# A two-layer graph kernel: when row tiles of the last product are finished, and its last transposes in two halves

## The chip, the cores and the metric

The kernel runs on one core of a Trainium2 chip. The metric is device microseconds of one execution; the median of five runs is compared. All data are float32.

## The reference

Two layers over 3327 nodes with 512 features, and one dense matrix `adj` (3327 x 3327):

```python
# layer 0
h = relu(layernorm(x))
q, k, v = h @ Wq.T + bq, h @ Wk.T + bk, h @ Wv.T + bv
x = x + softmax(q @ k.T / sqrt(512) + adj + adj) @ v
# layer 1
h = relu(layernorm(x))
A2 = adj + eye
d = diagonal(A2) ** -0.5
temp = A2 @ h @ W.T
x = x + relu((d[:, None] * A2 * d[None, :]) @ temp)
```

The kernel works out its three large products, (softmax weights) @ h, A2 @ h and A2 @ temp, each as a product of a (3328 x 3328) matrix and a (3328 x 512) one.

## The kernel before, in words

**Tiles.** Rows are padded to 26 tiles of 128. The rows of a result are held in two *strips*: strip 0 has row tiles 0 to 13, strip 1 has 14 to 25; half of a strip (7 or 6 tiles) is `y` = 0 or 1. The 512 feature columns are two halves `z` of 256.

**A product** (three of them, `g` = 0, 1, 2; the change is in the last) is done in two nested levels of a seven-product scheme in the manner of Strassen. The outer level has the seven products of `ORDER = ("p5", "p1", "p6", "p7", "p2", "p3", "p4")`. Each outer product goes over strip 0, then strip 1, and each strip over seven *steps*: `t` = 0 to 5, two tiles of the contraction at once, then `t` = `None`, the odd thirteenth. In the code, `number_of(g, n, s, t)` is the number of a step, with `n` the place in `ORDER`: `n` = 4 is outer p2, 5 is outer p3, 6 is outer p4. A number `t` of 6 is the `None` step, and 7 runs on into the next strip's first step.

Inside a step, `Step.multiply` (L770) issues seven inner products, also called p1 to p7, each into a PSUM bank of its own (`ROLE` has the bank numbers), in the order p6, p7, p5, p2, p3, p4, p1 for `t` = 0 and p1 first otherwise; two matmul records each in the profile, so 14 a step (L782). The `None` step issues p2, p3, p4 and p8 (8 records, L774), and p8 uses p1's bank. `four_sums` (L173 to L175, VectorE) makes the sums of the left operand two steps ahead; `make` (L748, L180 to L183) makes those of the right operand three steps ahead.

**Gathers.** At the end of a strip, VectorE takes the banks' content out: `first` (L810 to L814) after `t` = 5, `rest` (L827 to L830, or L824 for the very last one) at the `None` step, and `settle` (L838 to L843) adds the result to the buffers `ct` of the regions that it belongs to. The next strip's first step needs those banks again.

**Finishing a row tile.** `finish` (L919) transposes the tile's blocks of `ct` on TensorE (L927, four for 512 columns, two for 256) into bank 3, applies the relu with the row's scale on ScalarE (L929), adds the residual `xr` on VectorE (L930) and stores the tile from GpSimd's queue (L92). `finish_load` (L907, L910) fetches `xr`, on ScalarE's DMA queue, one step ahead. `xr` and the output tile come from rings of four buffers. When a tile can be finished follows from the scheme: the second halves (`z` = 1) of tiles 20 to 25 are complete after outer p7, tiles 0 to 6 after outer p3's strip 0, 14 to 19 after its strip 1, 7 to 13 after outer p4's strip 0, and the first halves of 20 to 25 only after the last step of all.

**What sets the order.** The order is written out by hand: `between[k]` holds what is emitted after step `k`, `within[k]` what is emitted after the fourth of its seven products. `in_order` keeps VectorE, TensorE, GpSimd, ScalarE and SyncE each to the order of emission, DMA issues included. `run` (L1012) emits, for one step: the loads of the step three ahead; the products, with `within` in their middle; at a `None` step `rest`; the sums for two steps ahead; after `t` = 5 `first`; after `None` `settle`; then `between`. In the last full step of all, `first` is emitted in the middle, ahead of `within`.

Of the kernel before, what the change touches and what calls it, by code (L numbers as in the profile page):

```python
# [15 lines left out]
P = 128  # L16
# [31 lines left out]
def graph_layers_kernel(  # L48
# [28 lines left out]
    nc = tc.nc  # L77
    N = out.shape[0]
    NP, D = x.shape
    DC = D // P  # L80
# [9 lines left out]
    def store(dst, src, n, queue=nc.gpsimd):  # L90
        for a, z in pieces(n):
            queue.dma_start(dst[a:z], src[a:z])  # L92
# [16 lines left out]
    def bank(k, name):  # L109
        return banks.tile([P, BW], F32, name=name, tag=f"bank{k}")  # L110
# [11 lines left out]
    @contextmanager  # L122
    def in_order(*engines):

        traced = nc.cur_bb.bb.instructions
        before = traced[-1]
        yield
        begin = next(k for k in reversed(range(len(traced))) if traced[k] is before) + 1
        last = {}
        for ins in traced[begin:]:  # L130
            if ins.engine in engines:
                if ins.engine in last:
                    tc.add_manual_dep(ins, last[ins.engine].name,
                                      mybir.DependencyInfo(mybir.DependencyClass.NoSync, mybir.DependencyReason.DATA),
                                      reason="in_order")
                last[ins.engine] = ins
# [5 lines left out]
    ident = const.tile([P, P], F32, name="ident")  # L142
# [88 lines left out]
    class Chain:  # L231
# [32 lines left out]
        @staticmethod  # L264
        def finish():
            if Chain.before:
                Chain.before()
            Chain.before = None
# [34 lines left out]
    ps = [bank(k, "mm") for k in range(DC)]  # L303
# [4 lines left out]
    for r in range(DC):  # L308
        for z in range(2):
            turned = -scale if r < 2 and z == 0 else scale  # L310
# [241 lines left out]
    with in_order(*(e.engine for e in (nc.vector, nc.tensor, nc.gpsimd, nc.sync))):  # L552
# [9 lines left out]
        k = len(steps)  # L562
# [16 lines left out]
    ROLE = {"p1": 0, "p6": 2, "p7": 4, "p5": 6, "p2": 7, "p3": 1, "p4": 5, "p8": 3}  # L579

    def seven():
        return {r: bank(ROLE[r], r) for r in ("p6", "p7", "p5", "p2", "p3", "p4", "p1")}
# [82 lines left out]
    cts = {}  # L665

    def set_up():

        free = [view(k, j)[:, 2 * m : 2 * m + 2] for k, j in ((2, 2), (3, 0), (3, 1), (3, 2)) for m in range(2)]
        free = [f.rearrange("p a w -> p (a w)") for f in free] + [mid(k, [P, H[0]], f"ct{k}") for k in range(10)]  # L670
        for s in range(2):
            cts[s] = [[free.pop()[:, : H[s]] for d in range(DC)] for y in range(2)]
        cts["to"] = [free.pop() for k in range(2)]
# [33 lines left out]
    class Right:  # L707
# [9 lines left out]
        def rows(self, dst, h, z):  # L717

            for k, i in enumerate(self.its):
                src = rowd[self.g][ROW[h * HALF + i]]  # L720
                nc.sync.dma_start(dst[:, k], src if z is None else src[:, z * E : (z + 1) * E])
# [31 lines left out]
    class Step:  # L753
# [8 lines left out]
        def sums(self):  # L762
            for a, d in self.diagonals:
                nc.vector.tensor_add(a, a, d)
            if self.t is None:
                return
            self.o = o_ring3()[:, :, : Q[self.s]]
            four_sums(self.o, self.a.rearrange("p k y w -> p (k y) w"))
# [16 lines left out]
    flags = []  # L785

    class Gather:
# [28 lines left out]
                for o, c, op in zip(self.parts(self.regions[2]), (c11, c12, c21, c22), (ALU.add, ALU.subtract, ALU.add, ALU.add)):  # L816
                    nc.vector.tensor_tensor(o, o, c, op=op)

        def rest(self, ps):
            p = {k: ps[k][:, : self.width] for k in ("p2", "p3", "p4", "p8")}  # L820
            if self.last:
                flags.append(nc.values_load(bad, min_val=0, max_val=1))
                for o, k in zip(self.parts(self.regions[2]), p):
                    nc.vector.tensor_add(o, o, p[k])  # L824
                return
            c11, c12, c21, c22 = self.parts(self.to)
            nc.vector.tensor_add(c11, c11, p["p2"])  # L827
            nc.vector.tensor_sub(c12, p["p3"], c12)
            nc.vector.tensor_add(c21, c21, p["p4"])
            nc.vector.tensor_add(c22, c22, p["p8"])  # L830
# [14 lines left out]
    def where(i):  # L845

        s = int(i >= STRIPS[1])
        return (s, *divmod(i - STRIPS[s], HT[s]))
# [63 lines left out]
    def last_load(i):  # L912

        xr = xr_last([P, 2, E], "xr")
        for k in range(2):
            xrs[i + k] = xr[:, k]
            nc.scalar.dma_start(xr[:, k], x1d[i + k][:, 0:E])

    def finish(i, z=(0, 1), spot=None, queue=nc.gpsimd):  # L919

        s, y, k = where(i)
        n = min(P, N - i * P)
        c0, c1 = z[0] * E, (z[-1] + 1) * E
        xr = xrs[i]
        pt = bank(ROLE["p8"] if spot is None else spot, "pt")
        for d in range(c0 // P, c1 // P):
            nc.tensor.transpose(pt[:, d * P : (d + 1) * P], cts[s][y][d][:, k * P : (k + 1) * P], ident)  # L927
        o = (out_ring if spot is None else out_last)([P, D], "r")
        nc.scalar.activation(o[:, c0:c1], pt[:, c0:c1], AF.Relu, scale=sd[:, i : i + 1])  # L929
        nc.vector.tensor_add(o[:, c0:c1], o[:, c0:c1], xr[:, c0:c1])  # L930
        store(out[i * P : i * P + n, c0:c1], o[:n, c0:c1], n, queue)
# [7 lines left out]
    def number_of(g, r, s, t):  # L939
        return ((g * len(ORDER) + r) * 2 + s) * len(every) + t  # L940

    def at(k, what, *args):
        between.setdefault(k, []).append((what, args))

    early = []
    for g in range(3):
        for n, r in enumerate(ORDER):
            for t, e in enumerate(every):
                k = number_of(g, n, 0, t)
# [9 lines left out]
    for n, job in enumerate(jobs):  # L959
        k = k0 + n * (k1 - k0) // len(jobs)  # L960
# [3 lines left out]
    def rows(g, k, i, *z):  # L964

        if g == 0:
            at(k - 2, attend_load, i)
            at(k, attend, i)
            at(k + 1, attended, i)
        elif g == 1:  # L970
            at(k, temp, i)
        else:
            at(k - 1, finish_load, i, *z)
            at(k, finish, i, *z)
# [3 lines left out]
    for g in range(2):  # L978
        k = number_of(g, 5, 1, 2)
# [4 lines left out]
            k += 1  # L984
    within = {}
    for (n, s, t), its in {
# [3 lines left out]
    }.items():  # L990
        for i, when in zip(its, (between, within)):
            if i is not None:
                k = number_of(2, n, s, t)
                at(k - 1, finish_load, i)
                when.setdefault(k, []).append((finish, (i,)))
    for t, i in enumerate(range(20, NT)):
        rows(2, number_of(2, 4, 0, t), i, (1,))
    for n, i in enumerate(range(20, NT, 2)):
        at(number_of(2, 6, 1, 2) + n, last_load, i)
    for k, what in ((1, totals), (2, prepare), (6, prepared), (8, judge), (9, judged)):  # L1000
# [9 lines left out]
    banks_of, gathers = {}, {}  # L1010

    def run(k):  # L1012
        step = steps[k]
        if k + 3 < len(steps):
            steps[k + 3].load()
        if step.t == 0:
            banks_of.update(seven())
        if not cts:
            set_up()
        if step.t is None:  # L1020
            banks_of["p8"] = bank(ROLE["p1"], "p8")
        t, sums = step.t, steps[k + 2].sums if k + 2 < len(steps) else tuple
        if t == PAIRS - 1:
            gathers[step.r, step.s] = Gather(step.r, step.s, k == len(steps) - 2)
        gatherer = gathers.get((step.r, step.s))
        for j, _ in enumerate(step.multiply(banks_of)):
            if j == 3 and t == PAIRS - 1 and gatherer.last:
                gatherer.first(banks_of)
            for what, args in within.get(k, ()) if j == 3 else ():
                what(*args)  # L1030
        if t is None:
            gatherer.rest(banks_of)
        sums()
        if t == PAIRS - 1 and not gatherer.last:
            gatherer.first(banks_of)
        if t is None:
            gatherer.settle()
        for what, args in between.get(k, ()):
            what(*args)

    with in_order(*(e.engine for e in (nc.vector, nc.tensor, nc.gpsimd, nc.scalar, nc.sync))):
        for k in range(len(steps)):
            run(k)
        for n, i in enumerate(range(20, NT)):
            finish(i, (0,), (0, 2, 4, 6, 7, 1)[n], (nc.gpsimd, nc.sync)[n % 2])
    return flags[0]

@with_exitstack
# [373 lines left out]
```

## Time and profile before

| | us |
|---|---|
| median of 5 runs | 2212.73 (2212.05 to 2215.41) |
| the profiled execution | 2213.48 |
| its span in the profile | 2211.6 |
| outer p2, p3 and p4 of the last product | from about 1985 to 2195 |
| last matmul starts; last DMA issue | about 2194.8; 2199.8 |

The profile is of one execution. PE is TensorE's matmuls, PEld its weight loads, DVE is VectorE, ACT ScalarE, POOL GpSimd, SP SyncE; a q behind the name is the engine's queue of DMA issues. A line of the timeline gives start and length in us, engine, source line, operation, output and inputs, shapes, the number of instructions, and in brackets how long the engine had been idle and what ended that. A line of the table by stretches gives for one stretch of time the busy time of PE, PEld, DVE, ACT and POOL, then TensorE's granted clock (1.00 is full), the busy share of the DMA engines and the GB/s that they moved.

### The profile page before, as it was taken

What the parts mean: (1) busy time and instruction counts of PE and PEld (TensorE: products, weight loads), DVE (VectorE), ACT (ScalarE), POOL (GpSimd) and SP (SyncE); (2) the same over time, 40 slices, a digit from 0 to 9 for tenths busy, and PEclk for the clock granted to TensorE, in tenths of its full rate; (3) what the DMA queues carried; (4) which work ended last, traced back from release to release, by engine and by line L of the source; (5) the groups of instructions that cost most, each with busy time, mean ns of one, the idle gap of its engine ahead of it and who ended that gap; (6) DMA issues with size and microseconds to landing.
All of it is one profiled execution on the core that took longest, in us unless ns stands there. A gap on an engine that the chain in (4) does not pass through costs nothing.

```text
span 2211.6 us, 20973 instructions
## 1 busy us (share of the span) xinstructions
PE 2176.7 (98%) x6268; PEld 1167.8 (53%) x6268; DVE 1627.7 (74%) x3103; ACT 231.0 (10%) x335; POOL 357.4 (16%) x551
## 2 busy tenths in 40 slices
PE   9999999999999999999999999999999999999997
PEld 6555555455555555555454555555545555555554
DVE  6369888888877788877777778886645358777776
ACT  5311121112110000000011000000000000000011
POOL 5233333333321000001222100000000000000001
PEclk9999999999999999999999999999999999999999
DMA  7568888888969898888787899876645458765685
GB/s 288 186 218 300 291 299 285 303 282 312 344 212 321 307 373 298 280 291 314 253 307 266 305 350 353 282 272 201 215 140 188 130 187 302 241 201 182 209 300 170
DMA packets 246682, 583.68 MB, mean 264 GB/s; under 512 B 34768, under 2 KB 106270, under 8 KB 246558
## 3 DMA queue, kind: packets, MB, share of 16 engines
q1 hardware_dynamic: 192270, 399.28, 54.5%
q0 software_dynamic: 44928, 167.49, 19.9%
q10 hardware_dynamic: 9360, 15.47, 2.1%
q8 instruction: 52, 0.85, 0.2%
q14 instruction: 72, 0.59, 0.1%
HBM read 414.28 MB, written 167.85 MB: 263 GB/s over the span
## 4 chain that ended last, share of the span: by engine, by line
PE 88%; DVE 5%; DMA 3%; issue 3%; POOL 1%; SPq 0%; ACT 0%; ACTq 0%; POOLq 0%; DVEq 0%
PE p L782 52%; PE Y L454 13%; PE p L874 7%; PE Z L454 6%; PE p L774 5%; PE X L454 3%; PE Y L347 1%; DVE part L173 1%; DMA b<-row 1%; DMA xt<-in_x_dram 0%; DMA g<-in_adjT_dram 0%; DVE part L174 0%; PE pt L927 0%; DMA p<-g 0%; PE Z L347 0%
## 5 line engine op out<-in xcount | busy, mean ns | idle before, releaser
L782 PE MATMUL p<-part,b 128*128 128x448 f32 (+1 forms) x3528 | 1253.7, 513 | 6.4 <-DVE part L174 4.9
L782 PEld LDWEIGHTS p<-part,b 128*128 128x128 f32 x3528 | 668.4, 190 | 571.0 <-issue 308.3
L173 DVE TENSOR_TENSOR part<-part 128x896 f32<-128x896 f32 (+1 forms) x252 | 257.0, 1020 | 94.9 <-PE p L782 43.9
L454 PE MATMUL Y<-qt,hp 128*128 128x448 f32 (+1 forms) x832 | 309.9, 515 | 4.3 <-DVE g L458 3.3
L454 PEld LDWEIGHTS Y<-qt,hp 128*128 128x128 f32 x832 | 158.4, 191 | 139.7 <-issue 73.5
L454 PE MATMUL Z<-qt,hp 128*128 128x384 f32 (+1 forms) x416 | 162.5, 513 | 0.0
L175 DVE TENSOR_TENSOR part<-part,part 128x448 f32<-128x448 f32 (+1 forms) x219 | 129.5, 591 | 16.9 <-DVE part L174 0.9
L174 DVE TENSOR_TENSOR part<-part,part 128x448 f32<-128x448 f32 (+1 forms) x219 | 129.5, 591 | 7.4
L774 PE MATMUL p<-part,b 128*128 128x448 f32 (+1 forms) x336 | 124.2, 513 | 0.0
L874 PE MATMUL p<-w,ct 128*128 128x512 f32 x272 | 123.5, 593 | 0.5 <-DVE part L886 0.5
L454 PEld LDWEIGHTS Z<-qt,hp 128*128 128x128 f32 x416 | 78.8, 190 | 67.4 <-issue 37.2
L458 DVE SCALAR_TENSOR_TENSOR g<-g,Y 128x384 f32<-128x384 f32 (+1 forms) x156 | 91.3, 586 | 29.1 <-PE Y L454 27.8
L868 POOL DMA_DIRECT2D sum<-job x52 | 28.4, 547 | 501.1 <-DVE job L865 283.5
L811 DVE TENSOR_TENSOR part<-p,part 128x384 f32<-128x384 f32 (+1 forms) x33 | 19.3, 586 | 108.0 <-PE p L782 107.4
L774 PEld LDWEIGHTS p<-part,b 128*128 128x128 f32 x336 | 63.6, 190 | 53.8 <-issue 32.4
L810 ACT COPY part<-p 128x384 f32<-128x384 f32 (+1 forms) x33 | 16.6, 503 | 684.3 <-PE p L782 683.5
L874 PEld LDWEIGHTS p<-w,ct 128*128 128x128 f32 x272 | 51.5, 190 | 59.7 <-issue 51.9
L454 PE MATMUL X<-qt,hp 128*128 128x384 f32 (+1 forms) x208 | 81.1, 512 | 0.0
L461 ACT ACTIVATE g<-g 128x768 f32<-128x768 f32 (+1 forms) x48 | 43.0, 896 | 355.1 <-DVE g L458 297.8
L446 POOL DMA_DIRECT2D sum<-o x52 | 36.9, 709 | 222.8 <-DVE o L440 154.1
L874 PE MATMUL p<-w,part 128*128 128x512 f32 x144 | 65.7, 592 | 0.0
L92 POOL DMA_DIRECT2D out_dram<-r x30 | 16.2, 542 | 304.0 <-DVE r L930 268.9
(165 smaller groups left out, 1878.7 us busy)
## 6 DMA issues: line engine op xcount, KB each, us to landing
part<-sum SPq DMA_DIRECT2D x104, 448.0 KB, 5.0
part<-p SPq DMA_DIRECT2D x91, 448.0 KB, 6.3
part<-sum SPq DMA_DIRECT2D x104, 384.0 KB, 3.4
part<-p SPq DMA_DIRECT2D x91, 384.0 KB, 4.3
part<-in_adjT_dram SPq DMA_DIRECT2D x78, 448.0 KB, 4.9
b<-row SPq DMA_DIRECT2D x234, 128.0 KB, 4.9
part<-in_adjT_dram SPq DMA_DIRECT2D x78, 384.0 KB, 3.7
g<-in_adjT_dram SPq DMA_DIRECT2D x52, 448.0 KB, 4.6
```

Source lines behind the costliest of these rows:

```text
L173: nc.vector.tensor_add(o[:, 0:2], g[:, 0:4:3], g[:, 1:2].to_broadcast([P, 2, g.shape[-1]]))
L174: nc.vector.tensor_add(o[:, 2], o[:, 1], g[:, 0])
L175: nc.vector.tensor_add(o[:, 3], o[:, 2], g[:, 2])
L347: nc.tensor.matmul(ps[:, :w], M[B[name]][:, c, o * P : (o + 1) * P], hp[k][:, A[name], c], start=start and c == 0, stop=c == 1, skip_group ...
L446: nc.gpsimd.dma_start(self.to(sumd)[:, 0:2], self.o)
L454: nc.tensor.matmul(ps[:, :wd], h_of(self.t, name, k), qt[B[name]][:, k], start=start and k == 0, stop=k == 1, skip_group_check=True)
L458: nc.vector.scalar_tensor_tensor(a[n], a[n], 2.0, ps[:, :wd], op0=ALU.mult, op1=ALU.add if sign > 0 else ALU.subtract)
L461: nc.scalar.activation(g[1], g[1], AF.Exp, **({"bias": pad} if self.t == HALF - 1 else {}))
L774: yield nc.tensor.matmul(ps[("p2", "p3", "p4", "p8")[k]][:, :w], b[:, z], a[:, 0, y], start=k == 3, stop=True)
L782: yield nc.tensor.matmul(ps[r][:, :w], b[:, i], m, start=self.t == 0, stop=self.t == PAIRS - 1 and r in ("p1", "p5", "p6", "p7"))
L868: nc.gpsimd.dma_start(sumd[self.s][self.j][:, 2 + self.k], self.a)
L874: nc.tensor.matmul(ps, cts[s][y][d][:, k * P : (k + 1) * P], w[d], start=d == 0, stop=d == DC - 1)
```

## The change

Three edits, all in the last product.

1. The second halves of row tiles 20 to 25 are finished two steps later: at outer p2's strip 0 after steps 2 to 5 and the `None` step, and after the first step of strip 1.
2. The other tiles are finished at other steps. Row tiles by step, with the one after the bar `within` the step and the others after it:

| outer product, strip | before | after |
|---|---|---|
| p3, strip 1 | t2: 0, t3: 1, t4: 2, t5: 3 | t1: 0, t2: 1, t3: 2, t4: 3 \| 4, t5: 5 \| 6 |
| p4, strip 0 | t0: 4, t1: 5, t2: 6 \| 17, t3: 14 \| 18, t4: 15 \| 19, t5: 16 | t1: 14, t2: 15 \| 16, t3: 17 \| 18, t4: 19 |
| p4, strip 1 | t2: 7 \| 8, t3: 9 \| 10, t4: 11 \| 12, t5: \| 13 | t1: \| 7, t2: 8 \| 9, t3: 10 \| 11, t4: 12 \| 13 |

3. The transposes of the last six first halves are taken out of `finish`. `rest` can now do a part of its additions: p2 and p3 first, then the transposes of tiles 20 to 22 (the 384 columns that those two additions complete), then p4 and p8, then the transposes of tiles 23 to 25. The banks that they go to are in the order in which the gather lets go of them: p6, p7, p5, p2, p3, p1, where before it was p1's bank first.

```diff
-        def rest(self, ps):
+        def rest(self, ps, names=("p2", "p3", "p4", "p8")):
             p = {k: ps[k][:, : self.width] for k in ("p2", "p3", "p4", "p8")}
             if self.last:
-                flags.append(nc.values_load(bad, min_val=0, max_val=1))
                 for o, k in zip(self.parts(self.regions[2]), p):
-                    nc.vector.tensor_add(o, o, p[k])
+                    if k in names:
+                        nc.vector.tensor_add(o, o, p[k])
                 return
...
+    def turned(i, z, spot):
+        s, y, k = where(i)
+        pt = bank(spot, "pt")
+        for d in range(z[0] * DC // 2, (z[-1] + 1) * DC // 2):
+            nc.tensor.transpose(pt[:, d * P : (d + 1) * P], cts[s][y][d][:, k * P : (k + 1) * P], ident)
+        return pt
+
+    turned_last = {}
+
+    def turn_last(i):
+        turned_last[i] = turned(i, (0,), LAST[i - 20])
+
+    LAST = tuple(ROLE[p] for p in ("p6", "p7", "p5", "p2", "p3", "p1"))
...
-        pt = bank(ROLE["p8"] if spot is None else spot, "pt")
-        for d in range(c0 // P, c1 // P):
-            nc.tensor.transpose(pt[:, d * P : (d + 1) * P], cts[s][y][d][:, k * P : (k + 1) * P], ident)
+        pt = turned(i, z, ROLE["p8"]) if spot is None else turned_last[i]
...
-        (5, 1, 2): (0,), (5, 1, 3): (1,), (5, 1, 4): (2,), (5, 1, 5): (3,),
-        (6, 0, 0): (4,), (6, 0, 1): (5,), (6, 0, 2): (6, 17), (6, 0, 3): (14, 18), (6, 0, 4): (15, 19), (6, 0, 5): (16,),
-        (6, 1, 2): (7, 8), (6, 1, 3): (9, 10), (6, 1, 4): (11, 12), (6, 1, 5): (None, 13),
+        (5, 1, 1): (0,), (5, 1, 2): (1,), (5, 1, 3): (2,), (5, 1, 4): (3, 4), (5, 1, 5): (5, 6),
+        (6, 0, 1): (14,), (6, 0, 2): (15, 16), (6, 0, 3): (17, 18), (6, 0, 4): (19,),
+        (6, 1, 1): (None, 7), (6, 1, 2): (8, 9), (6, 1, 3): (10, 11), (6, 1, 4): (12, 13),
     }.items():
...
     for t, i in enumerate(range(20, NT)):
-        rows(2, number_of(2, 4, 0, t), i, (1,))
+        rows(2, number_of(2, 4, 0, t + 2), i, (1,))
...
-        if t is None:
+        if t is None and gatherer.last:
+
+            flags.append(nc.values_load(bad, min_val=0, max_val=1))
+            for n, names in enumerate((("p2", "p3"), ("p4", "p8"))):
+                gatherer.rest(banks_of, names)
+                for i in range(20 + 3 * n, 23 + 3 * n):
+                    turn_last(i)
+        elif t is None:
             gatherer.rest(banks_of)
...
         for n, i in enumerate(range(20, NT)):
-            finish(i, (0,), (0, 2, 4, 6, 7, 1)[n], (nc.gpsimd, nc.sync)[n % 2])
+            finish(i, (0,), LAST[n], (nc.gpsimd, nc.sync)[n % 2])
```

The change adds no operation and takes none away: as many matmuls, transposes, additions, loads and stores are issued as before.

More of the change, by code (lines that the diff above doesn't have):

```diff
@@ L917, in last_load @@
             nc.scalar.dma_start(xr[:, k], x1d[i + k][:, 0:E])
+    def turned(i, z, spot):
[8 more added lines that the diff above has]
+    LAST = tuple(ROLE[p] for p in ("p6", "p7", "p5", "p2", "p3", "p1"))
     def finish(i, z=(0, 1), spot=None, queue=nc.gpsimd):
-        s, y, k = where(i)
         n = min(P, N - i * P)
```

## The prediction

> **What bounds the kernel now.** I read the page first: TensorE is busy all but everywhere, so only what removes or adds a TensorE wait, or shortens the tail behind its last matmul, can move the time.
> ```profile
> PE 2176.7 (98%) x6268; PEld 1167.8 (53%) x6268; DVE 1627.7 (74%) x3103; ACT 231.0 (10%) x335; POOL 357.4 (16%) x551
> ```
> Second, the waits of TensorE (us in total, times, longest), of which these three touch the steps that the change edits:
> ```profile
> PE pt L927 <- DVE part L840: 3.1, 2, 2.5
> PE p L782 <- DVE part L827: 1.5, 2, 1.3
> ...
> PE pt L927 <- DVE part L824: 1.1, 1, 1.1
> ```
> Here the transposes of row tile 20 wait for `settle` (L840), matmuls wait for a bank that `rest` has yet to read (L827), and the last transposes wait for the last additions (L824). I call them A, B and C. From 2130 to 2195 us TensorE waits for nothing.
>
> Third, the timeline of TensorE around A (start, length, then idle before in brackets):
> ```profile
> 1985.46 5.42 PE L782 MATMUL p<-part,b 128*128 128x448 f32 x14
> 1991.45 0.33 PE L927 MATMUL pt<-ident,part 128*128 128x128 f32 x1 [0.56 <-DVE part L840]
> 1994.30 0.47 PE L927 MATMUL pt<-ident,part 128*128 128x128 f32 x1 [2.52 <-DVE part L840]
> 1994.57 6.82 PE L782 MATMUL p<-part,b 128*128 128x448 f32 x14
> 2001.23 0.38 PE L927 MATMUL pt<-ident,part 128*128 128x128 f32 x2
> ```
> The 14 matmuls behind the wait take 6.82 us, the 14 before it 5.42. The table by stretches says why (TensorE's clock stands third from the right, at half):
> ```profile
> 1994.00:1997.40 3.40, 3.10 (x5) 1.62 (x6) 3.29 (x8) 0.47 (x1) 0.00 (x0) 0.50 0.42 142
> ```
> Fourth, VectorE and TensorE around B:
> ```profile
> 2117.18 0.69 DVE L930 TENSOR_TENSOR r<-r,xr 128x512 f32<-128x512 f32 x1 [3.53 <-DMA xr<-x1d]
> ...
> 2120.78 0.55 DVE L811 TENSOR_TENSOR part<-p,part 128x384 f32<-128x384 f32 x1
> ...
> 2124.61 0.68 DVE L930 TENSOR_TENSOR r<-r,xr 128x512 f32<-128x512 f32 x1
> 2125.22 0.55 DVE L827 TENSOR_TENSOR part<-part,p 128x384 f32<-128x384 f32 x1
> ```
> ```profile
> 2122.06 2.42 PE L782 MATMUL p<-part,b 128*128 128x448 f32 x6
> 2125.82 1.40 PE L782 MATMUL p<-part,b 128*128 128x448 f32 x3 [1.34 <-DVE part L827]
> ```
> VectorE stood 3.53 us in front of row 2's addition (L930), because `xr` had not landed, and everything queued behind it came late. The landing times of that load, issued by ScalarE's queue, between 2104 and 2121 us:
> ```profile
> DMA to landing us min/median/max: 6.1/6.2/7.2
> ```
> Fifth, the tail:
> ```profile
> 2194.25 1.94 DVE L824 TENSOR_TENSOR part<-part,p 128x384 f32<-128x384 f32 x4
> ```
> ```profile
> 2196.25 1.53 PE L927 MATMUL pt<-ident,part 128*128 128x128 f32 x12 [1.14 <-DVE part L824]
> ```
>
> **A: rows 20 to 25, second half, two steps later.** Undisturbed, these transposes follow each other at 5.48 us (2001.23, 2006.71). Row 20's were due 5.48 - 0.22 us after the step's start at 1985.46, at 1990.7; the next came at 2001.23. That is 10.5 us for a step of 5.48: 5.0 lost, of which 3.1 is idle, 1.5 the halved clock, the rest the stretched transposes. Two steps later `settle` (done at 1994.25) is long past. What is late next: the product p6 of the step after the next needs L174 of its own sums; that ended at 1996.83 and would be wanted at 1996.75, so 0.1 is given back. The six additions, stores and loads move along (0.42 us of VectorE each); in the steps they move to VectorE idled 1.7 to 5.1 us, and the two that cross into the next strip fall ahead of sums that had 2 us to spare. **A: -4.9.**
>
> A rule of the Trainium skill bears on this: "TensorE: Matmul & The Clock Gate", Part 1, puts the fall to half clock behind an idle window of about 3.4 us, and its oscillation section asks for no idle gap above that. This trace is stricter. Elsewhere one gap of 2.91 us was enough:
> ```profile
> 585.00:588.00 3.00, 0.16 (x1) 0.00 (x0) 1.01 (x2) 0.00 (x0) 0.00 (x0) 0.94 0.75 253
> 588.00:591.00 3.00, 2.94 (x5) 1.71 (x6) 2.83 (x6) 1.09 (x2) 1.27 (x2) 0.50 1.05 347
> ```
> By the rule the idle part alone would come back (A = -3.3); by the row 4.9 does. The row decides. But the page also calls the window free-running, so other executions may lose the clock or not: -3.3 and -4.9 are A's ends.
>
> **C: the tail.** Three edits. Row 13 no longer finishes inside the last full step, so its addition (0.6 us, at 2193.65, right ahead of L824) is gone from VectorE there. The additions p2 and p3 now free the first six transposes, which start behind the last matmul (about 2195.0) and not at 2196.25; p4 and p8 end 0.1 to 0.2 us after those six, and ScalarE, which takes 0.36 us a row (2.30 for six), hides that. The other order of banks makes no bank late: those of p6, p7 and p5 are read before `rest` begins. Whatever follows (relus, additions, stores, their landing) only moves forward. Less than nothing is excluded by order, more than 1.3 by TensorE's last matmul. **C: -1.3.** The verdict's load is ahead of the additions in both, at no cost.
>
> **B: rows 0 to 19.** The transposes' sum is the same (0.44 us a row), only their places move. Seven rows, not four, now finish in p3's second strip. I lay TensorE out from its start at 2090.63, with 4.52 us a step (14 records of 0.323): row 0 at 2099.7, row 1 at 2104.6, row 2 at 2109.6; step 4 starts at 2110.0, with row 4 in its middle at 2112.6 and row 3 at 2115.0; step 5 starts at 2115.4, with row 6 at 2118.0 and row 5 at 2120.4; the last step starts at 2120.8; p4's first step at 2123.4, and its product p2 at 2125.65.
>
> The loads: rows 3 and 4 are issued behind row 2's relu (a load follows its transposes by 0.69: 2104.18, 2104.87), at 2110.3 and 2110.7, rows 5 and 6 at 2115.65 and 2116.1. Row 4's and row 6's additions stand *ahead* of their step's sums on VectorE and are ready for relu after less than 4 us, but their loads need more: with 6.2 us row 4 goes at 2116.9, and behind it `make` (1.65) and row 3 (0.6); row 6 then goes at X = 2122.3.
>
> What is queued behind row 6: sums, `first`, `make`, row 5, `rest`. The trace of before has that very sequence: from L930 at 2117.18 to the end of L811 4.15 us, to the end of L827 8.6. Waiting for it is TensorE: bank p6 is free at X + 4.15, bank p2 at X + 8.6.
> - Floor: X = 2119.3, the end of row 6's relu. p6 waits 0.05, p2 2.2: 2.3, against 1.34 today: +0.95.
> - Ceiling: landing in 7.2 us, the worst shown. X = 2123.3; p6 waits 4.05, p2 2.1: 6.2, and with a halved clock (1.5, as in A) 7.7: +6.3.
> - Taken: X = 2121.7. The DMA engines are full here (345 GB/s from 2104 to 2124), which speaks for 6.2; but SyncE's queue holds a `rows` load that waits for VectorE's `make` (L735), so a late VectorE also thins the loads around row 6, and a pair of row loads landed in 5.3 and 5.8 at 2135. 5.6 lies between. p6 waits 2.45, p2 2.15: 4.6. **B: +3.3.** Gaps of 2.45 and 2.15 are shorter than those that halved the clock; I count none.
>
> Behind that, TensorE and VectorE are late together. In p4's first strip the first step has no row now and the second has one for two; I find L174 0.1 us ahead of its matmul in the third step (0.6 today), so no further wait. The loads that SyncE has behind L735 come some 5 us later and had 10 to spare. p4's second strip has VectorE to spare and loads landing in 3.0: nothing.
>
> **Sum.** -4.9 - 1.3 + 3.3 = -2.9. The profiled execution took 2213.48 (span 2211.6), the median is 2212.73; taken from the median, **2209.8 us**.
>
> **The rivals.**
> 1. *Loads land early* (5 us or less; VectorE catches up between rows 4 and 6): B falls to +1 to +2.3, the sum to -5.2 to -3.9: 2207.5 to 2208.8. For it: rows 0 to 2 are out of the way one step sooner. Against: no load in this stretch landed under 6.1. Chance 0.3.
> 2. *The slower side: the addends of rows 4 and 6 hold VectorE.* Two pairs add 512 KB to full engines, at 392 GB/s (2116 to 2120) 1.3 us: landing 8.5, X = 2124.6, waits 7.5, halved clock 1.5: B = +7.7, the sum +1.5: 2214.2. It decides from a landing of about 7.0 us with the clock lost (8.5 without). For it: the 3.53 above is this wait, now twice. To pass 0.2% it would need over 11 us. Chance 0.15.
> 3. *The split doesn't bite*: if p4's addition waits for the first six transposes, which read the same buffers, the second six start 1.0 us later, of which ScalarE's pace hides 0.2: C = -0.5, total 2210.6. Against: in this trace loads go into one half of a buffer while the other is in use. Chance 0.1.
> The likeliest has the remaining 0.45.
>
> About 0.2% (4.4 us) is what a measurement of this kernel can tell from no change. Faster by more asks for a time under 2208.3: rival 1 and an edge of the likeliest, 0.33. Slower by more: the far end of rival 2, 0.08. Within: 0.59. The range, 2206.8 to 2214.0, reaches from rival 1 with a landing at the floor to nearly rival 2, and takes in A's two ends.
>
> **What would show it.** A: no wait of `pt` for L840 and no clock of 0.50 near 1994. C: the last transposes start within 0.2 us of the last matmul. B: VectorE waiting for `xr` before rows 4 and 6, then TensorE waiting twice (for L811, then L827) at the start of p4; their sum is 4.6. Wrong would be: a wait of under 2 there (B too dear), or one of `pt` elsewhere.

## The result and the profile after

The changed kernel took 2210.06 us in the median of 24 runs (2206.78 to 2214.55), the kernel before 2212.6 in the median of 44 beside them: ratio 0.9989, 95% interval 0.9983 to 0.9994. That is 2.5 us, or 0.1%; the forecast was 2.9. The profiled execution took 2212.58 with a span of 2210.4.

In the changed kernel the transposes stand at L923, the relu of a row tile at L940 and its addition at L941. The waits of TensorE from 1970 us to the end:
```profile
PE p L782 <- DVE part L811: 4.0, 1, 4.0
PE p L782 <- DVE part L827: 0.2, 1, 0.2
PE pt L923 <- ACT r L940: 0.2, 1, 0.2
```
The waits A (L840) and C (L824) are gone. B has changed its name, from L827 to L811, and is three times as long.

**A.** The timeline of TensorE where row 20's transposes used to wait:
```profile
1986.20 16.21 PE L782 MATMUL p<-part,b 128*128 128x448 f32 x42
2002.24 0.38 PE L923 MATMUL pt<-ident,part 128*128 128x128 f32 x2
```
42 matmuls, three steps, in one piece: no idle, no slow stretch.

**B.** VectorE in outer p3's last steps and p4's first:
```profile
2115.72 0.69 DVE L941 TENSOR_TENSOR r<-r,xr 128x512 f32<-128x512 f32 x1 [7.35 <-DMA xr<-x1d]
...
2119.71 0.69 DVE L941 TENSOR_TENSOR r<-r,xr 128x512 f32<-128x512 f32 x1 [1.04 <-DMA xr<-x1d]
...
2123.30 0.55 DVE L811 TENSOR_TENSOR part<-p,part 128x384 f32<-128x384 f32 x1
```
The first line is row 4's addition, which kept VectorE waiting for 7.35 us; the second is row 6's, which cost another 1.04. L811, which frees the first bank, came that much later. The loads of `xr`, issued between 2100 and 2116 us:
```profile
DMA to landing us min/median/max: 4.1/6.3/8.0
```
The 8.0 is row 4's. TensorE then:
```profile
2123.91 4.19 PE L782 MATMUL p<-part,b 128*128 128x448 f32 x6 [4.02 <-DVE part L811]
2128.34 8.54 PE L782 MATMUL p<-part,b 128*128 128x448 f32 x22 [0.24 <-DVE part L827]
```
Six records take 4.19 us where they took 2.42, since the clock is halved behind the wait (third figure from the right):
```profile
2124.60:2128.00 3.40, 3.40 (x5) 1.24 (x4) 3.30 (x9) 0.00 (x0) 0.00 (x0) 0.50 0.60 197
```
**C.** The last additions (VectorE), and the last transposes (TensorE):
```profile
2194.91 2.00 DVE L824 TENSOR_TENSOR part<-part,p 128x384 f32<-128x384 f32 x4
```
```profile
2196.15 1.58 PE L923 MATMUL pt<-ident,part 128*128 128x128 f32 x12
```
The transposes now run beside the additions and follow the last matmul without a wait.

**Where the time went.** The `None` steps (L774) cut the trace into stretches that hold the same work in both kernels. From the starts of their matmuls in the timeline, in us:

| kernel | outer p2: 1982.88 to 2053.47 before | p3 strip 1 and p4 strip 0: 2087.62 to 2159.18 before | last `None` step to the end: from 2192.36 before |
|---|---|---|---|
| before | 70.59 | 71.56 | 19.2 |
| changed | 65.83 | 76.80 | 16.8 |
| changed, again | 65.83 | 76.67 | 16.6 |
| A alone | 65.84 | 70.13 | 18.6 |
| split alone | 70.81 | 71.17 | 19.3 |
| table alone | 70.79 | 76.64 | 19.3 |
| A and split, old table | 65.83 | 71.59 | 19.4 |
| loads earlier | 65.82 | 74.25 | 16.9 |
| four rows | 65.83 | 70.35 | 17.1 |
| four rows, again | 65.83 | 70.75 | 17.0 |
| split, row 13 moved | 71.95 | 70.35 | 17.0 |
| split, other buffers | 70.55 | 71.87 | 17.3 |

(With four rows one row's transposes, 0.44 us, fall behind the middle stretch; they are added to it here.) The stretches between are alike: 34.15 for p3's strip 0, 33.17 to 33.18 for p4's strip 1, 33.61 there with four rows. So the change is -4.8 + 5.2 - 2.4, nearly -2 in the profiled execution, and 0.7 us that its trace loses upstream of all this leave the -1.2 between the spans.

### The profile page after: what moved, and what is told of

It reads as the page before. It is cut to its first block, busy times and chain, and to the rows that moved or that the text cites. A ratio compares the mean times of both kernels' runs of the same rounds, so it can differ in the third digit from the quotient of the medians.

```text
span 2210.4 us, 20971 instructions
## 1 busy us (share of the span) xinstructions
PE 2179.9 (99%) x6268; PEld 1168.8 (53%) x6268; DVE 1628.0 (74%) x3103; ACT 231.0 (10%) x335; POOL 357.0 (16%) x551
## 4 chain that ended last, share of the span: by engine, by line
PE 87%; DVE 4%; DMA 4%; issue 3%; POOL 1%; SPq 0%; ACT 0%; ACTq 0%; POOLq 0%; DVEq 0%
PE p L782 52%; PE Y L454 12%; PE p L874 7%; PE Z L454 6%; PE p L774 5%; PE X L454 3%; DMA g<-in_adjT_dram 1%; PE Y L347 1%; DMA b<-row 1%; DVE part L173 1%; DMA xt<-in_x_dram 0%; POOL rstd L200 0%; POOL row L324 0%; DMA rows<-t 0%; PE pt L923 0%
## 5 line engine op out<-in xcount | busy, mean ns | idle before, releaser
L175 DVE TENSOR_TENSOR part<-part,part 128x448 f32<-128x448 f32 (+1 forms) x219 | 129.5, 591 | 16.6 <-DVE part L174 0.5
L774 PE MATMUL p<-part,b 128*128 128x448 f32 (+1 forms) x336 | 124.2, 513 | 0.0
L811 DVE TENSOR_TENSOR part<-p,part 128x384 f32<-128x384 f32 (+1 forms) x33 | 19.3, 586 | 106.8 <-PE p L782 106.6
L774 PEld LDWEIGHTS p<-part,b 128*128 128x128 f32 x336 | 63.7, 190 | 54.1 <-issue 32.4
L810 ACT COPY part<-p 128x384 f32<-128x384 f32 (+1 forms) x33 | 16.6, 503 | 677.6 <-PE p L782 677.2
```

The source lines that it names most:

```text
L175: nc.vector.tensor_add(o[:, 3], o[:, 2], g[:, 2])
L774: yield nc.tensor.matmul(ps[("p2", "p3", "p4", "p8")[k]][:, :w], b[:, z], a[:, 0, y], start=k == 3, stop=True)
```

## The experiments

My theory was that the three parts add up: A gains about 4, the table of row tiles loses 3 to 5, the tail gains about 1.3. The rival: the table costs nothing in the median, and A and the tail are worth only the 2.5 us seen. Every kernel here does all of the computation.

**A alone** (the kernel before with one line).
```diff
-        rows(2, number_of(2, 4, 0, t), i, (1,))
+        rows(2, number_of(2, 4, 0, t + 2), i, (1,))
```


> Only the second halves of tiles 20 to 25 move two steps later. Theory (the three parts add up: A about -4, the table about +3 to +5, the tail about -1.3): the wait of the transposes for L840 is gone with no other wait in its place, and the time falls by 3.3 (idle alone) to 4.9 us (with the halved clock), to about 2208.5. Rival (the table costs nothing, and the change's -2.5 is all that A and the tail are worth): about -1.3 us. The wait at the start of outer p4 (L827, 1.3 us) and the one at the end (L824, 1.1 us) stay as they were under both.

Measured 2207.17 against 2212.72: ratio 0.9978 (0.9970 to 0.9986), -5.5 us. The rival's -1.3 is outside the interval. The first column of the table gives A 4.8. The wait for L827 did not stay, as both had it: row 2's `xr` happened to land earlier and VectorE waited 2.06 for it, not 3.53; that is another 1.4 (second column). In the four other experiments with the old table that wait was 0.1, 1.0, 1.4 and 1.6 us. It follows the start of row 2's addition, which came 28.3, 29.2, 29.6 and 29.9 us behind the start of p3's `None` step before it (28.1 in A alone), and is no constant of the kernel.

**Split alone** (the kernel before with `turned`, `turn_last` and the new order of banks; row 13 still finishes in the last full step).

> Only the last transposes in two halves and their banks' order; row 13 still finishes in the last full step. Theory: the first six transposes start as soon as the p2 and p3 additions are done, about 1.0 us earlier relative to the last matmul than before, and the time falls by 1.0 us (row 13's addition, which stands ahead of those additions, keeps the other 0.3). Rival: p4's addition waits for the first six transposes, the second six start 1 us later, and only 0.5 us is gained.

2212.96 against 2212.72: ratio 0.9999 (0.9990 to 1.0007). Neither expectation was right: the transposes do start 1.3 us earlier (2193.41, with the last `None` step at 2190.83), and nothing comes of it. The timeline of ScalarE's relus:
```profile
2194.16 0.47 ACT L940 ACTIVATE r<-pt,sd 128x256 f32<-128x256 f32 x1 [4.38 <-PE pt L923]
2195.52 1.94 ACT L940 ACTIVATE r<-pt,sd 128x256 f32<-128x256 f32 x5 [0.88 <-PE pt L923]
```
Row 20's relu goes early, row 21's waits. The profile names TensorE for it, but row 21's transposes, 0.44 us behind the first, were long done. What came at the right time is the landing of row 13's store. Its issue on GpSimd's queue, and its time to landing:
```profile
2193.11 0.54 POOL L92 DMA_DIRECT2D out_dram<-r  x1 [4.79 <-DVE r L941]
```
```profile
DMA to landing us min/median/max: 2.3/2.3/2.3
```
2193.1 + 2.3 = 2195.4. Both rings of output tiles share buffers, and row 13's is row 21's. Two further kernels test that.

**Split, with row 13 alone moved.**
```diff
-        (6, 1, 2): (7, 8), (6, 1, 3): (9, 10), (6, 1, 4): (11, 12), (6, 1, 5): (None, 13),
+        (6, 1, 2): (7, 8), (6, 1, 3): (9, 10), (6, 1, 4): (11, 12), (6, 1, 1): (None, 13),
```


> The split tail alone, with row 13 alone moved out of the last full step (to the second step of that strip). Theory (in the split alone, row 21's relu waited for its output buffer until row 13's store had landed, 2.3 us after the last matmuls' start plus 2.3): the relus follow each other without that wait, VectorE's last addition ends 1.3 us earlier against the last None step than before, the end comes 1.3 to 2.4 us earlier. Rival (the tail is set by the stores' landing, whatever is ahead of it): the end stays 19.2 us behind the start of the last None step.

2209.32 against 2212.6: ratio 0.9985 (0.9979 to 0.9992), -3.3 us. The tail is 17.0 and not 19.2. (Its 71.95 for outer p2 is A's wait with the clock halved for two stretches of 3.4 us, not one.)

**Split, row 13 left, its buffer last in the ring of the last six.**
```diff
-    out_last = ring((half, 12), (half, 13), *spare[2:], (half, 14))
+    out_last = ring((half, 12), *spare[2:], (half, 14), (half, 13))
```


> The split tail alone, row 13 where it was, but the six last tiles take the output buffers in another order: row 13's comes last, for row 25. Theory (it is the buffer and not VectorE's time that undid the split): no wait of ScalarE for a store any more, VectorE's last addition 1.0 us earlier against the last None step, the end 1.0 to 2.1 us earlier. Rival (row 13's addition ahead of the last ones undoes it): nothing is gained, as in the split alone.

2210.28 against 2212.6: ratio 0.9990 (0.9983 to 0.9997), -2.3 us; the tail is 17.3. The relus follow each other:
```profile
2194.62 2.30 ACT L940 ACTIVATE r<-pt,sd 128x256 f32<-128x256 f32 x6 [4.42 <-PE pt L923]
```
One buffer's order is worth what the whole split is worth. Row 13's addition ahead of L824 is not what undid it.

**Table alone** (the kernel before with the new table; old second halves, old tail).

> Only the table of row tiles is the new one; A and the tail are as before. Theory: VectorE waits about 7 us in front of row 4's addition and again before row 6's, TensorE waits 4 us for L811 at the start of outer p4 in place of the 1.3 us for L827, and often loses the clock there: +3 to +5 us. Rival (the table costs nothing in the median): within 1 us of before.

2218.43 against 2212.72: ratio 1.0023 (1.0014 to 1.0033), +5.7 us. The rival falls. VectorE waited here as in the changed kernel:
```profile
2118.63 0.69 DVE L930 TENSOR_TENSOR r<-r,xr 128x512 f32<-128x512 f32 x1 [6.55 <-DMA xr<-x1d]
```
TensorE waited 4.2 for L811 and 0.5 for L827, with the clock halved behind it. Row 13, moved by this table too, gives the tail nothing without the split (19.3).

**A and split, old table.**

> The change with the old table: A and the split tail, rows 0 to 19 as before. Theory: both gains without the table's loss, -4.3 to -5.9 us, about 2207.5, faster than the changed kernel by 2 to 4 us. Rival (the table costs nothing): about -2.5 us, the same as the changed kernel.

2206.36 against 2212.72: ratio 0.9970 (0.9960 to 0.9981), -6.4 us, 3.7 under the changed kernel. That is a little more than expected, but the interval, -8.8 to -4.2 us, takes in most of the range. The tail's share is missing (19.4, since row 13 is where it was).

**Loads of rows 3 to 6 one step earlier** (the changed kernel with one line).
```diff
-                at(k - 1, finish_load, i)
+                at(k - (2 if 3 <= i <= 6 else 1), finish_load, i)
```


> The changed kernel with the residual loads of rows 3 to 6 issued one step earlier, so that they land before their additions are reached. Theory (the landing of rows 4 and 6 is what holds VectorE): the long waits for xr before rows 4 and 6 are gone or under 1 us, L811 is in time, TensorE keeps only a wait for L827 of about 2.2 us, and the time falls by 2 to 4 us below the changed kernel's, to about 2207. Rival (VectorE is simply overloaded by seven rows in one strip): TensorE still waits about 4 us at the start of outer p4, and the time is the changed kernel's.

2207.89 against 2212.3: ratio 0.9980 (0.9971 to 0.9989). The changed kernel beside it had 2210.61, so 2.7 us came back and the rival falls. TensorE at the start of outer p4:
```profile
2117.65 2.73 PE L782 MATMUL p<-part,b 128*128 128x448 f32 x6 [1.73 <-DVE part L811]
2122.09 4.40 PE L782 MATMUL p<-part,b 128*128 128x448 f32 x11 [1.70 <-DVE part L827]
```
3.4 us in two waits, and no halved clock. The theory was too hopeful in two points: L811 was still late, by 1.7 us, and VectorE still waited 3.5 us for row 4's `xr` and 1.5 for row 6's. The same loads took longer when they were issued earlier; the DMA engines' busy share was 0.94 there (2097 to 2113 us), as in the changed kernel (2100 to 2120):
```profile
DMA to landing us min/median/max: 6.6/7.5/10.4
```

**Four rows in p3's second strip** (the changed kernel with another table).
```diff
-        (5, 1, 1): (0,), (5, 1, 2): (1,), (5, 1, 3): (2,), (5, 1, 4): (3, 4), (5, 1, 5): (5, 6),
-        (6, 0, 1): (14,), (6, 0, 2): (15, 16), (6, 0, 3): (17, 18), (6, 0, 4): (19,),
-        (6, 1, 1): (None, 7), (6, 1, 2): (8, 9), (6, 1, 3): (10, 11), (6, 1, 4): (12, 13),
+        (5, 1, 1): (0,), (5, 1, 2): (1,), (5, 1, 3): (2,), (5, 1, 4): (3,),
+        (6, 0, 1): (14, 4), (6, 0, 2): (15, 5), (6, 0, 3): (16, 6), (6, 0, 4): (17, 18),
+        (6, 1, 1): (19, 7), (6, 1, 2): (8, 9), (6, 1, 3): (10, 11), (6, 1, 4): (12, 13),
```


> The changed kernel with another table: rows 0 to 3 after steps 1 to 4 of p3's strip 1 and no row at its step 5; rows 4, 5, 6 move into p4's strip 0 and row 19 into its strip 1. Theory (a row that stands between the sums and the gather on VectorE is what TensorE pays for): no wait at the start of outer p4 at all, and with A and the tail the time falls by 5.5 to 7.5 us below before, to about 2206. Rival (the wait goes elsewhere): the rows that move into p4's strip 0 make sums late there, TensorE waits for L174 in p4's steps 2 to 4, and the gain over the changed kernel is under 1.5 us.

2203.95 against 2212.3: ratio 0.9954 (0.9940 to 0.9968), -8.4 us. TensorE at the start of outer p4 has no wait worth a line, and the clock stayed full:
```profile
2116.07 8.83 PE L782 MATMUL p<-part,b 128*128 128x448 f32 x22
```
TensorE waited for nothing in the rest of p4 either. Both kernels, before and changed, are beaten. Once more, in another set:

> The version with four rows in p3's second strip once more: about 2204, 8 us under before, with no wait of TensorE over 0.2 us from outer p2 to the end.

2205.02 against 2212.6: ratio 0.9964 (0.9954 to 0.9974), -7.6 us. One wait of 0.5 us for L827 came up, more than the 0.2 expected.

**The changed kernel, again.**

> The changed kernel, unchanged, beside the two others: about 2210, with one wait for L811 of 3 to 4 us at the start of outer p4 after a wait of VectorE for xr of about 7 us.

2210.61 against 2212.3: ratio 0.9993 (0.9985 to 1.0001), -1.7 us, which by itself is not told from no change. TensorE waited 3.96 for L811, behind a wait of VectorE of 7.2, as expected.

## Why the prediction was right, point by point

The number held (2209.8 forecast, 2210.06 measured), and each part has the sign that was forecast. But two of the three terms were too small, in opposite directions, B by 1.9 and C by 1.1. That these errors nearly cancel is luck: the sum is better than its parts.

- **A, -4.9: right.** 4.8 by the stretches, 5.5 between medians when done alone. That the row of the trace decides, and not the idle window of about 3.4 us that the Trainium skill gives ("TensorE: Matmul & The Clock Gate", Part 1), was right as well: the clock was halved at this wait, 0.56 and 2.52 us of idle, in all five profiles that still have it, and in none without it.
- **B, +3.3: right in mechanism, too small.** The stretches say +5.2, the table alone +5.7 between medians. The term that failed is X, the start of row 6's addition. The second strip of p3 starts 4.0 us earlier here (2086.61, not 2090.63), so the measured 2119.71 is 2123.7 on the prediction's scale; 2121.7 was taken, and the ceiling was 2123.3. First, row 4's load took 8.0 us and not the 6.2 worked with, longer than any that the trace of before showed, and left 0.9 late; that alone kept VectorE from row 6 until 2118.7. Second, row 6's load took only 4.1, but its issue was late: 2115.5, where 2116.1 less 4.0 is 2112.1. The prediction took the issue to follow a relu at once. The chain of releases in the changed kernel, followed back from that load, shows what held it (start, length, what):
```profile
2106.91 8.49 DMA rows<-t
2115.40 0.02 issue
2115.43 0.02 ACTq L910
2115.44 0.04 issue
2115.48 4.10 DMA xr<-x1d
```
ScalarE's queue (ACTq, L910) issued row 6's load when a load of `rows` had landed, which SyncE's queue had issued 8.5 us before. In the two other profiles with this table and these loads it was a `rows` load too, of 6.9 and 7.5 us. So a slow landing on another queue held row 6's load back, a wait that the prediction had put at nothing.
- **The two waits' sum: right, once X is right.** Bank p2 is free at X + 8.6. With the measured X the prediction's own sum gives 2123.7 + 8.6 - 2125.65 = 6.7 us of waiting, less 1.34 is +5.3, and the stretches say +5.2.
- **"Gaps of 2.45 and 2.15 ... I count none": wrong, but this cost nothing.** The wait became one of 4.0 us, and the clock was halved in each of the three profiles with this table and these loads. Six records took 1.8 us longer (4.19 for 2.42), and the second wait was that much shorter (0.24 for the 2.15 forecast), since VectorE's L827 ends it, which TensorE's clock did not delay. In the changed kernel, again, the clock was half for 6.8 us instead of 3.4, and the stretch is the same (76.67 and 76.80).
- **C, -1.3: right in sign, wrong in how.** The transposes start 1.3 us earlier, as worked out (2196.25 - 2192.36 = 3.89, now 2196.15 - 2193.57 = 2.58). But the step "whatever follows only moves forward" overlooked the buffers: row 13's addition was worth 0.3 there for its time on VectorE, while its store held row 21's buffer, and without moving it the split was worth nothing. With both, the end comes 2.4 earlier, though the prediction held more than 1.3 to be excluded. The other 1.1 is in the last store of GpSimd's queue: it landed 4.2 us after its issue before and in the split alone, 3.1 to 3.2 in the changed kernel and in the two kernels with row 13 or its buffer moved, and the end lies 8.0 to 8.1 behind that landing in all five. Why it landed sooner was not tested.
- **The rest of B's list held.** In p4's first strip nothing waits behind that start, the loads behind L735 were in time, and p4's second strip gave and took nothing (33.18 before, 33.17 after).
- **Rival 1** (early landing) did not come. **Rival 2** came in its mechanism, a landing of 8.0 and a halved clock, but at 5.2 and not 7.7. Its X was 0.9 later than the measured one, and it added 1.5 for the halved clock to a second wait that the halved clock in fact took the place of; so it did not turn the sign. **Rival 3** fell: p4's addition did not wait for the first six transposes; the four additions and the twelve transposes each run in one piece (2.00 and 1.58 us).

## What to carry to other kernels

An addition that waits for a load, placed on an in-order engine ahead of the work that frees a bank, hands the load's landing time to TensorE: count such waits by the longest landing when the DMA engines are full, not by the median, look whether the load's issue itself waits for an earlier transfer, and put nothing of the kind between the last sums and a gather. A halved clock costs only where TensorE, and not the engine it waits for next, sets the pace. When work is pulled forward, look at which buffers the next consumers take: the last link was a store's landing here, and the order of one ring was worth as much as the restructured tail. And take a change of several parts apart before judging it: this one, worth 0.1%, held a gain of 5, a loss of 5, and a gain of 2 that neither of its halves had alone.

## What the runs showed of the hardware

The clock was halved by shorter waits than the prediction supposed. Both kernels have, far upstream of the change, one wait of 1.93 us. Before (TensorE, then the stretch behind it):
```profile
882.08 10.27 PE L782 MATMUL p<-part,b 128*128 128x384 f32 x31 [1.93 <-DVE part L174]
```
```profile
882.20:885.60 3.40, 3.40 (x11) 2.08 (x12) 3.26 (x5) 0.00 (x0) 0.00 (x0) 1.00 0.44 123
```
After:
```profile
881.12 11.31 PE L782 MATMUL p<-part,b 128*128 128x384 f32 x29 [1.93 <-DVE part L174]
```
```profile
882.10:885.60 3.50, 3.50 (x7) 1.88 (x6) 3.22 (x6) 0.00 (x0) 0.00 (x0) 0.51 0.39 100
```
The same wait, one clock halved for 3.4 us and one not. It was halved in seven of the twelve profiles. In each profile the changes of the clock, those of this kind and the others, lie on a grid of 3.41 us; laid on it, the wait fell whole into one cell in the seven (1.92 to 1.93 us of idle time), and in four of the others a boundary cut it (before: 1.05 and 0.87; the closest 1.78 and 0.15). In the twelfth 1.92 lay in one cell and the clock stayed, so the limit is near there. (A wait of 2.52 us at 605.86 in the second profile with four rows, cut into 1.54 and 0.98, left the clock whole as well.) Where TensorE sets the pace, each such event costs 1.7 us, half of 3.4. It differs between executions of one kernel: the changed kernel lost the clock here in one profile and not in the other. So it can be one reason why single runs of one kernel spread over 7 us, though no run here shows how much of that it makes. A gain of 2 us is seen in medians of many runs, or in the stretches of a profile, and not in two spans.
